# A two-layer graph network on one core: the first layer's table split twice as fast, products from block 12, more early work for GpSimd, the last unit in two

## The chip, the core and the metric

The kernel runs on one core of a Trainium2 chip. A core has five engines that run side by side and meet through semaphores: TensorE (PE; its weight loads are listed as PEld), VectorE (DVE), ScalarE (ACT), GpSimd (POOL) and SyncE (SP, which here only issues transfers). Transfers run on 16 DMA engines. Computing engines read and write the on-chip memory; TensorE's results go to a small memory of accumulators (PSUM).

The metric is the device time of one execution in microseconds (us); lower is better. The profile is one execution on the chip, recorded instruction by instruction.

## What is computed

The input is a graph of 6,250 nodes with 128 features each and 200,000 edges, sorted by destination. Two layers follow each other; each begins with a layer norm and a relu and adds its result to `x`:

```python
h = jnp.maximum(_layernorm(x), 0.0)
# layer 0: attention over the edges
z = h @ W                                   # 128 features in 8 heads of 16
e = leaky_relu(el[src] + er[dst])           # el, er: one number per node and head
a = exp(e - segment_max(e, dst)[dst])
x = x + segment_sum(z[src] * a, dst) / segment_sum(a, dst) + bias
h = jnp.maximum(_layernorm(x), 0.0)
# layer 1: messages weighted by a small network on the edge features
s, v = h[:, :32] @ W_up_s, h[:, 32:] with W_up_v
w0..w3 = split(silu(silu(edge_feats @ A1 + b1) @ A2 + b2) @ A3)
m = concat(s[src]*y_s*w0, (v[src].y_v)/R3*w3, s[src]*y_v*w1, v[src]*y_s*w2)
x = x + (segment_sum(m, dst) / 10) @ W_out
```

The part that matters for the change is `z[src]` in layer 0 and `s[src]`, `v[src]` in layer 1: for each of the 200,000 edges a row of a table is fetched, by an index that only the data tell.

## The kernel before

**Tiles and blocks.** Nodes lie in `NX` = 50 tiles of 128. Edges lie in `TU` = 1563 tiles of 128, sixteen tiles to a block (`KB` = 16), so there are `NB` = 98 blocks; the last has 11 tiles. Since the edges are sorted, the destinations of a block fall into a window of 128 nodes; the sum over edges is a product with a one-hot matrix of the destinations.

**Three ways to fetch rows.** The table of layer 0 is `t0` (136 numbers a row), that of layer 1 is `t1` (128 numbers), both in the chip's main memory.
- Most edge tiles are fetched with an indirect transfer that GpSimd issues (`gather`, line 839): one instruction for 128 rows. Those of a block go into one of five buffers (`buffer()`), which are used in turn; a gather into a buffer has to wait until the block that was there has been read.
- In every third block, tile 15 is fetched row by row by SyncE (`rows_by_row`, line 1154): 128 small copies, whose number per step is paced by `rows_until`.
- In "dense" blocks (`dense` in layer 0, every fourth block, `dense1`, in layer 1) tile 14 (`KD`) is not fetched but computed: a one-hot matrix of the sources (`ends_to`, line 1300) times the whole table (`rows_of` of layer 0, line 1313). For that the table lies on chip, each number split into three bf16 parts (`t0s`). Three tiles of the table at a time (`TS` = 3) are loaded by SyncE (`asked(k)`, line 1275) into one of two buffers `zr` and split by VectorE (`split(k)`, lines 1228 to 1231), k from 0 to 16. The product takes 17 one-hot matrices by 3 parts, 51 matmuls; `taken` (lines 1319 and 1321) picks the result. Its tiles are taken in `order`.

**Prologue.** Line numbers 880 to 1005. GpSimd first gathers rows of the input `x` itself for the first edge tiles (`gather_x`, line 905): `KX` = 25 tiles. Meanwhile the other engines norm the 50 node tiles in ten groups and write `t0` (`rows_of` of the prologue). There the groups' normalising step (line 960) runs on VectorE and ScalarE, except that in two of the groups five tiles are normed by GpSimd (`late`). VectorE then computes whether the edges are evenly spread (`fok`, line 936); every engine reads that number and branches. After the branch `rows_of` runs a second time, over the 25 gathered x tiles, and computes their table rows directly, so these 25 edge tiles need no gather from `t0`.

**Layer 0.** One step `g` a block, in an order written out by hand for TensorE, VectorE, ScalarE and SyncE (`manual_schedule`): gathers of block g+3 are issued, the logits of block g computed, one-hots of blocks g+1 and g+2 prepared, the sums of block g-1 taken, finished node tiles normed and multiplied for layer 1 and written to `t1`. A copy `t1z` of `t1` is written too, with zeros for the last `NL` = 3 node tiles. In step g stand `asked(g - 2)` near the begin and `split(g - 3)` at the end.

**The seam.** Layer 1's gathers need all of `t1`, whose last tiles come at the very end of layer 0. So the first `NE` = 24 edge tiles of layer 1 are gathered early from `t1z`, and the rows of the last three node tiles are added afterwards by a product with a one-hot (`late_ends`, lines 1868 and 1872; `late_rows`, lines 1883 and 1886), four edge tiles at a time.

**Layer 1.** Units of up to four edge tiles (`us`). For each: the small network on TensorE and ScalarE, the messages on VectorE (`messages`, lines 1807 to 1816), the sums on TensorE (line 1824). The last block's 11 tiles make units of 4, 4 and 3. After the last unit come the last two node tiles' products and the write to `out`.

The lines that name the changed numbers:

```python
NL, NE = 3, 24
TS = 3
dense = set(range(-(-NX // TS) + 4, NB - 4))     # 21 .. 93
us = [{"b": b, "k0": k0, "m": min(4, KT[b] - k0)}
      for b in range(NB) for k0 in range(0, KT[b], 4)]
```

Of the kernel before, what the change touches and what calls it, by code (L numbers as in the profile page):

```python
# [13 lines left out]
OP = mybir.AluOpType  # L14
# [15 lines left out]
KB = 16  # L30
# [711 lines left out]
def tile_even_edges(  # L742
# [28 lines left out]
    nc = tc.nc  # L771
    NX = xp.shape[0] // P
    TU = n_tiles
    TG = -(-TU // P)
    NB = -(-TU // KB)
# [27 lines left out]
    src_col = keep.tile([P, TU], I32, name="fsrc")  # L803
    z_first = keep.tile([P, KB, ZW], F32, name="fz_first")
    ok_i = keep.tile([1, 1], I32, name="fok")
    KX = KB + 9
    z_second = keep.tile([P, KB, ZW], F32, name="fz_second")
    other = keep.tile([P, KB, ZW], F32, name="fz_other")
    flat = other.rearrange("p k f -> p (k f)")
# [46 lines left out]
    with tc.manual_schedule(engines={mybir.EngineType.PE, mybir.EngineType.DVE,  # L856
# [11 lines left out]
        xs = [fx.tile([P, n, P], F32, name=f"fxs{i}") for i, n in gx]  # L868
# [69 lines left out]
        def rows_of(gx, xs, fp, fp_ps, raw=None):  # L938

            mark = "e" if raw else ""  # L940
            NC = len(gx)
            mvs, rss, mrs, hs = {}, {}, {}, {}
            todo, done, outs, ers = [], [], [], []
            for k in range(NC + 3):
                if 0 <= k - 1 < NC:
                    rss[k - 1] = deviation(fp, mvs[k - 1], gx[k - 1][1], f"x{mark}{gx[k - 1][0]}")
                c = k - 2
                if 0 <= c < NC:
                    i, n = gx[c]
                    rs, mr = rss[c], mrs[c] = normal(fp, mvs[c], rss[c], n, f"x{mark}{i}")  # L950
                    h = hs[c] = fp.tile([P, 6, P], F32, name="fh")
                    for j in range(n):
                        by = (i + j) % 7
                        if by in ((2, 6) if c < NC - 2 else (2,)):
                            nc.scalar.activation(h[:, j, :], xs[c][:, j, :], AF.Identity,
                                                 bias=mr[:, j, :], scale=rs[:, j, :])
                        else:
                            late = by in (0, 3, 5) and NC - 4 <= c < NC - 2 and not raw
                            eng = nc.gpsimd if late else nc.vector
                            eng.tensor_scalar(h[:, j, :], xs[c][:, j, :], mvs[c][:, j, 0:1],  # L960
                                              rs[:, j, :], op0=OP.subtract, op1=OP.mult)
                if k == NC + 1 and not raw:
                    uneven_edges()
                for i, n, zt in ers:
                    nc.vector.tensor_copy(er_all[:, i : i + n, :], zt[:, :n, ZW:])
                ers = []
                if k >= 3:
                    i, n = gx[k - 3]
                    zt = raw[k - 3] if raw else fp.tile([P, 6, CW], F32, name="zt", bufs=4)
                    todo += [(k - 3, zt, j0, min(3, n - j0)) for j0 in range(0, n, 3)]  # L970
                while todo:
                    c, zt, j0, m = todo.pop(0)
                    p_t = fp_ps.tile([P, 4, P], F32, name="p_t")
                    for j in range(m):
                        nc.tensor.transpose(p_t[:, j, :], hs[c][:, j0 + j, :], ident)
                    h_t = fp.tile([P, 3, P], F32, name="h_t")
                    nc.scalar.activation(h_t[:, :m], p_t[:, :m], AF.Relu)
                    done.append((c, zt, j0, m, h_t))
                    while len(done) > (1 if k < NC + 2 or todo else 0):
                        c, zt, j0, m, h_t = done.pop(0)  # L980
                        p_z = fp_ps.tile([P, 3, CW], F32, name="p_z")
                        for j in range(m):
                            nc.tensor.matmul(p_z[:, j, :], h_t[:, j, :], w_ext, start=True, stop=True)
                        outs.append((c, zt, j0, m, p_z))
                        while len(outs) > (1 if k < NC + 2 or todo or done else 0):
                            c, zt, j0, m, p_z = outs.pop(0)
                            copy = nc.scalar.copy if c < NC - 2 else nc.vector.tensor_copy
                            w = ZW if raw else CW
                            copy(zt[:, j0 : j0 + m, :w], p_z[:, :m, :w])
                            i, n = gx[c]  # L990
                            if j0 + m == n and not raw:
                                to_table(t0, zt[:, :, :ZW], i, n, nc.sync)
                                ers.append((i, n, zt))
                                load(c)
                if k < NC:
                    i, n = gx[k]
                    mvs[k] = moments(fp, xs[k], n, f"x{mark}{i}")
            for i, n, zt in ers:
                nc.vector.tensor_copy(er_all[:, i : i + n, :], zt[:, :n, ZW:])
# [11 lines left out]
def even_edges(tc, v):  # L1011
    nc = tc.nc
    NX, TU, TG, NB, KT, MC = (v[k] for k in (
        "NX", "TU", "TG", "NB", "KT", "MC"))
# [5 lines left out]
    with ExitStack() as ctx:  # L1020
# [25 lines left out]

        NL, NE = 3, 24
        LATE = NX - NL  # L1050
        sv_of = {}
        iota = const.tile([P, P], F32, name="fiota")
# [9 lines left out]
        with tc.tile_pool(name="fbuild", bufs=1) as build:  # L1062
# [30 lines left out]
            for k, by in enumerate((-H, P - H, H)):  # L1093
# [4 lines left out]
                                    op0=OP.mult, op1=OP.add)  # L1098
# [11 lines left out]
            with tc.tile_pool(name="fat_ps", bufs=1, space=PSUM) as at_ps, \  # L1110
                    tc.tile_pool(name="fat_c", bufs=1) as at_c:
                col = at_c.tile([P, P], F32, name="fcol")
                n = NB - 1
# [83 lines left out]
        order = sorted(range(NR), key=lambda k: (k > 0, 2 * NR + k < NX, k))  # L1197
        half = (NR + 1) // 2
        TS = 3
        dense = set(range(-(-NX // TS) + 4, NB - 4))  # L1200
        dense1 = set(range(10, NB - 4, 4))

        ranges = []
# [34 lines left out]
        with tc.manual_schedule(engines=in_order), \  # L1238
# [23 lines left out]
            def asked(k):  # L1262

                i = TS * k
                if 0 <= i < NX:
                    n = min(TS, NX - i)
                    zr = asked.of[k] = l0d.tile([P, TS, ZW], F32, name="zr", bufs=2)[:, :n]
                    if i == 0:
                        nc.vector.memset(zr[:W0, 0, :], 0.0)
                        nc.sync.dma_start(zr[W0:, 0, :], t0[: P - W0, :])  # L1270
                        of = t0[P - W0 : n * P - W0]
                        nc.sync.dma_start(zr[:, 1:], of.rearrange("(j p) f -> p j f", p=P))
                    else:
                        of = t0[i * P - W0 : (i + n) * P - W0]
                        nc.sync.dma_start(zr, of.rearrange("(j p) f -> p j f", p=P))

            def split(k):
                if k in asked.of:
                    zr = asked.of.pop(k)
                    n = min(TS, NX - TS * k)  # L1280
                    in_three(t0s[:, TS * k : TS * k + n], zr, rest0[:, :n])
# [295 lines left out]
            for g in range(NG - 3):  # L1577
# [4 lines left out]
                    node_out(n)  # L1582
                for n in split_:
                    parts_out(n)
                asked(g - 2)
                if g % 2 == 0 and g // 2 + 2 < NX - 2:
                    node_rows(g // 2 + 2, 1)
                rows_until(rows, g + 1)
                c, b4 = cs[g], (cs[g - 1] if g else None)
# [64 lines left out]
                    sums(b4, 8)  # L1654
                if to:
                    rows_of(n2, 6, half - 6)
                split(g - 3)
                if g == 4:
                    ends_in_ranges(const)
                if g == NG - 4:  # L1660
# [74 lines left out]
        with tc.manual_schedule(engines=in_order), \  # L1735
# [192 lines left out]
            def dense_step(b, q):  # L1928
# [6 lines left out]
                if b in dense1:  # L1935
# [4 lines left out]
            blk = [{} for _ in range(NB)]  # L1940
            us = [{"b": b, "k0": k0, "m": min(4, KT[b] - k0)}
                  for b in range(NB) for k0 in range(0, KT[b], 4)]
            NU = len(us)

            def take_rows(b):
# [219 lines left out]
```

## Time and profile before

| | |
|---|---|
| median of 3 runs | 5950.58 us (5947.39 to 5958.39) |
| the profiled execution | 3749.37 us, of which the span from the first to the last instruction is 3747.6 us |
| mean granted TensorE clock in it | 0.936 of full speed |
| row copies of SyncE (line 1154) | 7808, of 0.5 KB |
| moved by DMA | 262.78 MB, 70 GB/s on average |

The profiled execution and the runs differ by 2201 us; every duration in this document that is read from a view belongs to the profiled execution.

How to read the views. The page gives for each engine its busy time and share of the span. Its second part cuts the span in 40 equal slices: a digit is the busy share in tenths; PEclk is TensorE's granted clock in tenths of full speed. A line of groups reads: source line, engine, operation, output<-input by the program's names, count | busy time, mean ns of one | idle time of the engine just before, and who ended it. A line of the timeline reads: start, duration, engine, line, operation, count, and in brackets the idle time before it and its releaser. "issue" means that nothing in the profile was waited for. An "SPq" entry is a transfer being issued, not its data moving.

### The profile page before, as it was taken

The page shows a single profiled execution, that of the slowest core. Times are in us where ns is not written, and L with a number is a line of the kernel's source. Part 1 is how long each engine was busy: PE and PEld are TensorE (multiplying, and loading weights), DVE is VectorE, ACT ScalarE, POOL GpSimd, SP SyncE. Part 2 cuts the span into 40 slices and gives each one's busy share as a digit, 9 for nine tenths or more (in the row PEclk, how much of TensorE's full clock was granted, in tenths as well). Part 3 has the DMA queues.
Part 4 walks back from the last instruction along what each step waited for, and adds up shares of the span by engine and source line. Part 5 has one row for each costly group of instructions (what it writes and reads, how often), then busy time and mean ns, then how long its engine had stood idle before and what let it go on. Part 6 is the DMA issues. An engine that isn't in the chain of part 4 may idle for free. (4 is left out here: it accounts for less than half of the span.)

```text
span 3747.6 us, 74803 instructions
## 1 busy us (share of the span) xinstructions
PE 3196.4 (85%) x19845; PEld 2474.1 (66%) x19845; DVE 2633.1 (70%) x6272; ACT 1406.0 (38%) x3638; POOL 2817.3 (75%) x2981
## 2 busy tenths in 40 slices
PE   4756788888888888888788899999999999999997
PEld 4655566666666666666666677777677777767775
DVE  7755666666666666666657777777777777777776
ACT  4432333333333333333334444444444444444443
POOL 7777777777777777777777777777777777777776
PEclk7766899999999999999799999999999999999999
DMA  6333332222222222222223222222222222222222
GB/s 167 75 78 79 71 68 67 68 69 68 68 68 68 68 68 67 69 69 67 71 70 95 69 64 64 64 64 64 64 64 64 65 63 64 65 63 64 63 68 52
DMA packets 212534, 262.78 MB, mean 70 GB/s; under 512 B 77425, under 2 KB 163921, under 8 KB 212097
## 3 DMA queue, kind: packets, MB, share of 16 engines
q0 software_dynamic: 95072, 200.78, 22.6%
q1 hardware_dynamic: 116592, 57.03, 5.7%
q8 instruction: 159, 2.61, 0.3%
q14 instruction: 279, 2.28, 0.2%
q10 hardware_dynamic: 432, 0.09, 0.0%
HBM read 236.19 MB, written 21.14 MB: 69 GB/s over the span
## 5 line engine op out<-in xcount | busy, mean ns | idle before, releaser
L839 POOL DMA_INDIRECT fz<-ft,fsrc x1750 | 1654.1, 945 | 539.5 <-issue 327.0
L1824 PE MATMUL p_u<-mj,s 128*128 128x256 f32 x3126 | 764.3, 388 | 87.5 <-DVE mj L1816 86.5
L1313 PE MATMUL p_x<-t0s,fz_first 128*128 128x408 bf16 (+1 forms) x3723 | 730.0, 346 | 0.0
L1824 PEld LDWEIGHTS p_u<-mj,s 128*128 128x128 f32 x3126 | 582.2, 192 | 215.6 <-DVE mj L1816 139.7
L839 POOL DMA_INDIRECT fz_other<-ft,fsrc x589 | 557.2, 946 | 179.6 <-issue 107.6
L839 POOL DMA_INDIRECT fz_second<-ft,fsrc x583 | 554.0, 950 | 178.3 <-issue 107.9
L1313 PEld LDWEIGHTS <-fz_first 128*128 128x128 bf16 x3723 | 361.5, 101 | 231.5 <-issue 17.4
L1791 ACT ACTIVATE p_w<-p_w,yb 128x64 f32<-128x64 f32 x1563 | 451.5, 289 | 117.3 <-PE p_w L1787 73.8
L1787 PE MATMUL p_w<-fa3p,h 128*128 128x256 f32 x1564 | 408.4, 384 | 0.0
L1787 PEld LDWEIGHTS p_w<-fa3p,h 128*128 128x128 f32 x1564 | 286.7, 193 | 114.5 <-issue 48.8
L1772 ACT ACTIVATE h<-p_h,fb 128x512 f32<-128x512 f32 x196 | 134.7, 687 | 585.8 <-PE p_h L1770 575.1
L1337 ACT COPY mk<-p_m 128x384 f32<-128x384 f32 (+1 forms) x99 | 47.4, 479 | 658.5 <-PE p_m L1333 651.6
L1427 PE MATMUL p_u<-fz,s 128*128 128x136 f32 x1846 | 272.9, 308 | 20.1 <-DVE fz L1422 20.1
L1427 PEld LDWEIGHTS p_u<-fz,s 128*128 128x128 f32 x1846 | 258.5, 216 | 23.8 <-DVE fz L1422 22.2
L1173 DVE TENSOR_TENSOR s<-p_i,fdloc 128x512 f32<-128x512 f32 x391 | 268.6, 687 | 3.8 <-ACT p_i L1766 3.8
L1173 DVE TENSOR_TENSOR s<-p_m,fdloc 128x512 f32<-128x512 f32 x391 | 266.2, 682 | 3.0 <-ACT mk L1337 2.7
L1770 PE MATMUL p_h<-ft,fa1p 128*128 128x128 f32 x1568 | 216.1, 282 | 56.5 <-DMA ft<-in_e_f_dram 56.3
L1770 PEld LDWEIGHTS p_h<-ft,fa1p 128*128 128x128 f32 x1568 | 208.7, 197 | 79.8 <-issue 55.7
L1348 ACT CAST d<-p_d 128x512 bf16<-128x512 f32 x391 | 229.3, 586 | 78.0 <-PE p_d L1346 34.2
L1378 DVE TENSOR_TENSOR_SCAN pe<-mk,pe 128x128 f32<-128x128 f32 x98 | 42.0, 428 | 290.8 <-PE pe L1293 271.6
L1777 ACT ACTIVATE h<-p_h,fb 128x512 f32<-128x512 f32 x196 | 134.7, 687 | 260.4 <-PE p_h L1774 260.4
L1811 DVE TENSOR_REDUCE vd<-vy 128x128 f32<-128x384 f32 x391 | 229.6, 587 | 0.0
(285 smaller groups left out, 4880.5 us busy)
## 6 DMA issues: line engine op xcount, KB each, us to landing
r<-ft SPq DMA_DIRECT2D x3968, 0.5 KB
r<-ft SPq DMA_DIRECT2D x3840, 0.5 KB
fz<-ft,fsrc POOLq DMA_INDIRECT x1750
fz_other<-ft,fsrc POOLq DMA_INDIRECT x589
fz_second<-ft,fsrc POOLq DMA_INDIRECT x583
fx<-x SPq DMA_DIRECT2D x47, 160.0 KB
ft<-in_e_f_dram SPq DMA_DIRECT2D x98, 64.0 KB
t1s<-fx SPq DMA_DIRECT2D x7, 576.0 KB
```

The costliest lines, as they stand in the source:

```text
L839: nc.gpsimd.indirect_dma_start(out=to[:, k, :width], out_offset=None, in_=table, in_offset=bass.IndirectOffsetOnAxis(ap=src_col[:, t : t + ...
L1173: nc.vector.tensor_tensor(s[:, :m], iota[:, None, :].to_broadcast([P, m, P]), dloc[:, t : t + m].unsqueeze(2).to_broadcast([P, m, P]), OP. ...
L1313: nc.tensor.matmul(c["p_x"][:, :m, :], c["oh", k // half][:, k % half, :], t0s[:, i::NR, s, :], start=k == 0 and s == 0, stop=k == NR - 1 ...
L1348: nc.scalar.copy(d[:, :m], p_d[:, :m])
L1427: nc.tensor.matmul(c["p_u"][:, :ZW], c["s"][k // 4][:, k % 4, :], c["z"][:, k, :], start=c["o"] + k == 0, stop=c["o"] + k == KT[c["b"]] - 1)
L1770: nc.tensor.matmul(p_h[:, q, :], a1p[:, q0 + q, :], c["ft"], start=True, stop=True)
L1772: nc.scalar.activation(c["h1"], p_h, AF.Silu, bias=b1)
L1777: nc.scalar.activation(h2, p_h, AF.Silu, bias=b2)
L1787: nc.tensor.matmul(w[:, k : k + n].rearrange("p k a u -> p (k a u)"), c["h2"][q // 4][:, q % 4, :], a3p[:, :n].rearrange("p k f -> p (k f) ...
L1791: nc.scalar.activation(w[:, k, ::2, :], w[:, k, ::2, :], AF.Copy, scale=c["yb"][:, k0 + k, 0:1])
L1811: nc.vector.tensor_reduce(vd, vy.rearrange("p t i u -> p t u i"), AX.X, OP.add)
L1824: nc.tensor.matmul(blk[b]["p_u"][:, :MW], u["s"][:, k, :], u["mj"][:, k, :], start=k0 + k == 0, stop=k0 + k == KT[b] - 1)
```

## The change

`KX` goes from 25 to 29 and `NE` from 24 to 28. In the prologue's normalising step the GpSimd branch is gone; VectorE does those five tiles. `dense` begins at block 12 instead of 21. To have the table ready, a step calls `asked` twice and `split` twice, with the same two indices, 2g-4 and 2g-3, so that a piece is loaded at the begin and split at the end of the same step. The last unit of layer 1, of three tiles, is cut into one of two tiles and one of one. Three operations of the gather count change with it: 1422 instead of 1435 gathers from `t0`, 28 instead of 24 from `t1z`, 1483 instead of 1487 from `t1`; and 29 instead of 25 gathers of x.

```diff
-    KX = KB + 9
+    KX = KB + 13
...
                         else:
-                            late = by in (0, 3, 5) and NC - 4 <= c < NC - 2 and not raw
-                            eng = nc.gpsimd if late else nc.vector
-                            eng.tensor_scalar(h[:, j, :], xs[c][:, j, :], mvs[c][:, j, 0:1],
-                                              rs[:, j, :], op0=OP.subtract, op1=OP.mult)
+                            nc.vector.tensor_scalar(h[:, j, :], xs[c][:, j, :], mvs[c][:, j, 0:1],
+                                                    rs[:, j, :], op0=OP.subtract, op1=OP.mult)
...
-        NL, NE = 3, 24
+        NL, NE = 3, 28
...
         TS = 3
-        dense = set(range(-(-NX // TS) + 4, NB - 4))
+        dense = set(range(-(-NX // TS // 2) + 3, NB - 4))
...
-                asked(g - 2)
+                for k in range(2):
+                    asked(2 * g - 4 + k)
...
-                split(g - 3)
+                for k in range(2):
+                    split(2 * g - 4 + k)
...
+            if us[-1]["m"] > 2:
+
+                n = us[-1]["m"] - 2
+                us[-1]["m"] = 2
+                us.append({"b": NB - 1, "k0": us[-1]["k0"] + 2, "m": n})
             NU = len(us)
```

## The prediction

> **What bounds the kernel now.** I read the page first: engine shares, the row of slices, the costliest groups. Then GpSimd's (POOL's) timeline around the prologue and the seam between the layers, the busy time in stretches of the first layer, VectorE's timeline inside one step, and the tail.
>
> From the page (the groups' columns are count | busy, mean ns | idle before, its releaser):
>
> ```profile
> span 3747.6 us, 74803 instructions
> PE 3196.4 (85%) x19845; PEld 2474.1 (66%) x19845; DVE 2633.1 (70%) x6272; ACT 1406.0 (38%) x3638; POOL 2817.3 (75%) x2981
> ...
> POOL 7777777777777777777777777777777777777776
> PEclk7766899999999999999799999999999999999999
> ...
> L839 POOL DMA_INDIRECT fz<-ft,fsrc x1750 | 1654.1, 945 | 539.5 <-issue 327.0
> ```
>
> TensorE's 85% is the larger share, but POOL's row is flat from end to end: the same 7 in every slice, whatever the other engines do. One gather takes 0.945 us and a fixed 0.30 us of issue follows. From 41.17 to 3733 us the gathers start every 1.25 us, and the waits of POOL show one gap over 1 us there, at the seam. There are 1435 gathers from the first table, 24 early ones and 1487 from the second by the program's loops (the page's groups hold 2938 of the 2946; a few records are missing): 2946 x 1.25 = 3682 us, the span but for the prologue (41), the tail (14) and a few long gathers. So in this execution POOL paces everything.
>
> POOL's timeline in the prologue and at the seam (start, duration, instruction, idle before):
>
> ```profile
> 22.70 0.94 POOL L905 DMA_INDIRECT fz_first<-in_e_xp_dram,frow  x1 [0.30 <-issue]
> 24.10 4.21 POOL L960 TENSOR_SCALAR fh<-fxs,mvx,rsx 128x128 f32<-128x128 f32 x5 [0.46 <-PE p_t L975]
> 28.47 1.03 POOL L905 DMA_INDIRECT fz_second<-in_e_xp_dram,frow  x1 [0.16 <-issue]
> ...
> 39.41 0.94 POOL L905 DMA_INDIRECT fz_second<-in_e_xp_dram,frow  x1 [0.30 <-issue]
> 41.17 0.98 POOL L839 DMA_INDIRECT fz_second<-ft,fsrc  x1 [0.82 <-issue]
> ```
>
> ```profile
> 1868.22 1.08 POOL L839 DMA_INDIRECT fz<-ft1z,fsrc  x1 [0.30 <-PE p_n L1481]
> 1869.61 0.94 POOL L839 DMA_INDIRECT fz<-ft1z,fsrc  x1 [0.31 <-issue]
> 1876.60 0.94 POOL L839 DMA_INDIRECT fz<-ft,fsrc  x1 [6.04 <-PE p_h L1868]
> ```
>
> The reader should see 4.21 us of layer norm inside POOL's stream, and 6.04 us in which POOL stands still after the 24th early gather, until the second table is whole.
>
> Busy time in a stretch without products and one with them (us, then busy and count of PE, PEld, DVE, ACT, POOL, then clock):
>
> ```profile
> 180.00:260.00 80.00, 46.03 (x318) 41.37 (x319) 48.90 (x113) 25.24 (x58) 60.47 (x65) 0.67 0.34 77
> 440.00:540.00 100.00, 89.47 (x695) 66.24 (x694) 68.14 (x142) 30.11 (x70) 75.62 (x80) 0.95 0.30 67
> ```
>
> POOL is busy 0.756 of both; TensorE goes from 0.58 to 0.89, its clock from 0.67 to 0.95. Inside a step before block 21, VectorE waits for gathered rows right after the table split:
>
> ```profile
> 363.36 0.58 DVE L1231 TENSOR_TENSOR t0s<-rest,t0s 128x408 bf16<-128x408 f32 x1
> 370.44 0.29 DVE L1369 TENSOR_TENSOR e_s<-fz,p_er 128x128 f32<-128x128 f32 x1 [6.50 <-DMA fz<-ft,fsrc]
> ```
>
> **The median is another matter.** The profiled execution took 3749.37 us (span 3747.6 and 1.8 around it); the median of the runs is 5950.58, 1.587 times as long, and no view says where the other 2201 us lie. I make the sum against 3749.37 and ask afterwards which engine can be the pace at 5950.
>
> **What the Trainium skill says.** "GPSIMD Engine Reference", section 4, names gathers with data-dependent indices as work for GpSimd alone, whose cores write the descriptors in software. The trace agrees: each gather holds POOL for 0.945 us. "SBUF — State Buffer", "Who interferes with whom", says that a VectorE tensor_scalar can enter a mode in which it locks GpSimd out of a shared port for the whole instruction. The moved layer norm is of that kind, but the gathers between 12.67 and 20.19 us, beside VectorE's own L960, take 0.94 to 0.98, so I charge nothing. "TensorE: Matmul & The Clock Gate", Part 1, says that TensorE's clock is half unless sustained activity releases it; the two stretches above, 0.67 and 0.95, agree.
>
> **The change part by part.**
>
> Products from block 12. The set of dense blocks goes from 21..93 to 12..93: nine blocks more take tile 14 from products with the split table instead of a gather. POOL loses 9 x 1.25 = 11.2 us. TensorE gains in each 51 matmuls of L1313 (730.0 us / 73 blocks = 10.0 us) and a spread; VectorE gains the one-hots L1300 (1.36 + 1.22) and the taking (3 x 0.36), 3.7 us. A dense block's POOL period is 14.67 gathers x 1.25 = 18.3 us; TensorE needs 0.895 of that, 16.4 us at clock 0.95, and in blocks 21 to 93 POOL never waits beside that same load. Hidden, if the clock is granted. Without that cover, at 0.67, it is 23.3 us a block: rival A.
>
> Split at double rate. Nothing is added in all: the same 17 pieces, of 4 x 0.58 us on VectorE, in steps 2 to 10 instead of 3 to 19. Per step 2.4 us come on top and fall into the 4 to 6.5 us wait shown above. A piece is now loaded and split in the same step. SyncE issues the load once the last step's splits are done (the issues at 117.0, 134.0, 154.3 show it), about 17 us before the split at the step's end, so it is there in time. On SyncE's queue the second load takes 0.41 us; behind it stand the row copies, 44 in 17.6 us, and between them the queue has free 2 to 3 us in every three steps. Hidden.
>
> Prologue. Five operations leave POOL: 24.10 to 28.47 becomes free, and four more x gathers (4 x 1.25 = 5.0) fill it. These end at 23.9 + 13 x 1.25 = 40.2 instead of 40.35, and four table gathers fewer follow: 5.0 us gained. VectorE takes the five at 0.34, pipelined 0.27: 1.4 us, so its verdict on the edges (ends at 37.25) comes at 38.6 and its last table copy as much later. The first table gather waits for both; at 41.17 there is room for the first, for the second perhaps not: I take 0 and keep 1 us. VectorE, ScalarE and TensorE norm four more x tiles and one more group, about 4 us, so block 0 starts 5 us later. What is late next is buffer reuse: block 6 overwrites block 1's buffer, free at 119.9, wanted at 133.1. After it: free at 125, wanted at 128. Three us are left; block 7 has 147 against 142 once the doubled splits are counted.
>
> Seam. Four more gathers need only the zero-padded table: 5.0 of the 5.7 us of extra wait are filled. The cost: one more round of late ends and rows, 16 matmuls of 0.275 (4.4 us) and VectorE's 3 x 0.74 + 0.69 = 2.9 us. Block 2's buffer was last read at 1967.4 and wanted again at 1984; the margin of 16 shrinks to about 5. Hidden.
>
> Last unit in two. The unit of three tiles takes VectorE 2.3 us after the last gather lands; in two it costs about 0.6 us more in instructions and leaves two matmuls instead of six behind. I take 0 (-0.5 to +0.5).
>
> Sum: 11.2 + 5.0 + 5.0 = 21.2 us off 3749.4, 3728.2 (-0.57%), with 16 to 22 as bounds.
>
> **Carried to the median.** If POOL is stretched to the longer run, a gather takes (5950 - 55)/2946 = 2.0 us; 13 gathers fewer are 26 us, and the seam has no wait left to fill, since 24 x 2.0 exceeds the 36 us from the last first-layer gather (1840) to the second table. If the excess is a constant, 21 us. By ratio, 34. I take 26: 5925 us; this case's own range is 5912 to 5936.
>
> **Rivals.**
>
> A, slower: TensorE is the pace. For it: busy 3196.4 at mean clock 0.936 is 2992 us at full clock, and twice that, at half clock, is 5984, within 1% of the median. Against it: the profile's clock. The place is blocks 12 to 20, and it decides once a dense block's 15.6 us (at full clock) exceed 18.3, at a clock under 0.85. If only those blocks stay at 0.67, each takes 23.3 instead of 19.6 us: 9 x 3.7 = 33, less the 10 of prologue and seam, +23 us, 5975. At half clock throughout, 9 x 10.0 x 0.95 x 2 = +171 at most; less what waits hide, about +150: 6100.
>
> B, no change: the row copies on SyncE are the pace of the longer run. There are 7808 of them, 0.40 us each here; at 0.76 they alone would fill 5950. The change removes none. For it: SyncE has little slack here. Against it: nothing shows it stretched. Time 5950, to 5945.
>
> C, given back: the buffer of block 1 isn't free (if block 0 starts 9 rather than 5 us late, POOL stands 1 to 5 us), the first table gather comes 1 us later, and the tail costs 0.5. Gain 15 in this execution's time, 5936.
>
> That the change doesn't do what it says: the table's last piece (tiles 48, 49) is split in step 10, and block 12's products with it come in step 11; I see no way for that.
>
> **How the numbers follow.** Forecast 0.58, C 0.06, B 0.11, A 0.25 (of it 0.09 near 5975, 0.16 higher). About 0.2% (12 us) is what a measurement of this kernel tells from no change: the forecast and C count as faster, 0.64, B as same with a little of A, 0.12, the rest slower, 0.24. The range reaches from the ratio's end, with a margin, over B and A's lower end: 5905 to 5995; A's upper end is left out.
>
> **What would show it.** Right: 1422 gathers from the first table, still one every 1.25 us, the first near 41, none standing over 1 us at the seam, the clock near 0.95 from about 220 us instead of 420, and the last gather 21 us earlier. Wrong: a gap on POOL at blocks 6 to 8; idle on POOL behind L1313 or L1427 in blocks 12 to 20; VectorE waiting on L1228 for a load; a profiled gain near 21 with a longer median, which would make A or B the pace of the timed runs.

## The result, and the profile after

The changed kernel takes 5976.21 us (median of 8 runs, 5956.22 to 5984.85); the kernel before took 5948.81 us (8 runs, the three from ahead of the prediction among them). The ratio is 1.0042, with a 95% interval of 1.0024 to 1.0060: slower by about 25 us, where 5925 us and a gain were forecast.

The profiled execution of before that the prediction rests on (3749 us) was not a luckier run of the same thing: this kernel takes about 3746 us on some chips and 5890 to 5960 us on others, and in each later comparison the kernel before keeps to one of the two paces. (Each chip was seen in one comparison only; on which chips the first profile and the first runs were made is not on record.) I call them the short and the long pace. The result above was measured at the long pace, the profile that I argued from at the short one.

From the page of the changed kernel (5984.85 us; groups: count | busy, mean ns | idle before, releaser):

```profile
span 5983.1 us, 75909 instructions
PE 3890.7 (65%) x20366; PEld 2776.4 (46%) x20366; DVE 2667.2 (45%) x6346; ACT 1393.8 (23%) x3643; POOL 2807.6 (47%) x2967
...
POOL 6344444444444444444444455555545555545552
PEclk7667777777777777777766888888888888888889
...
L839 POOL DMA_INDIRECT fz<-ft,fsrc x1740 | 1648.1, 947 | 1828.4 <-PE p_u L1425 654.5
```

A gather still takes 0.947 us. But GpSimd's row has fallen from 7 to 4, and the gathers of this group wait 1828 us instead of 540. The largest part with a name, 654 us, is for the first layer's sums (L1425) to give a buffer back. The gathers are not stretched; GpSimd stands still. So the two pages can't be set side by side, and the kernel before has to be profiled at the long pace first.

### The profile page after: what moved, and what is told of

It reads as the page before. It is cut to its first block, busy times and chain, and to the rows that moved or that the text cites. A ratio compares the mean times of both kernels' runs of the same rounds, so it can differ in the third digit from the quotient of the medians.

```text
span 5983.1 us, 75909 instructions
## 1 busy us (share of the span) xinstructions
PE 3890.7 (65%) x20366; PEld 2776.4 (46%) x20366; DVE 2667.2 (45%) x6346; ACT 1393.8 (23%) x3643; POOL 2807.6 (47%) x2967
## 3 DMA queue, kind: packets, MB, share of 16 engines
q8 instruction: 163, 2.67, 0.2%
## 5 line engine op out<-in xcount | busy, mean ns | idle before, releaser
L1311 PE MATMUL p_x<-t0s,fz_first 128*128 128x408 bf16 (+1 forms) x4182 | 1087.7, 398 | 495.5 <-issue 494.8
L1824 PE MATMUL p_u<-mj,s 128*128 128x256 f32 x3126 | 881.1, 430 | 334.7 <-DVE mj L1816 239.1
L1824 PEld LDWEIGHTS p_u<-mj,s 128*128 128x128 f32 x3126 | 651.9, 216 | 507.4 <-DVE mj L1816 285.4
L1311 PEld LDWEIGHTS <-fz_first 128*128 128x128 bf16 x4182 | 441.5, 110 | 945.8 <-issue 807.1
L1787 PE MATMUL p_w<-fa3p,h 128*128 128x256 f32 x1564 | 446.2, 412 | 0.6 <-issue 0.6
L1774 PE MATMUL p_h<-h,fa2p 128*128 128x512 f32 x392 | 247.2, 718 | 220.1 <-ACT h L1772 217.0
L1787 PEld LDWEIGHTS p_w<-fa3p,h 128*128 128x128 f32 x1564 | 315.4, 212 | 146.2 <-issue 106.9
L1770 PE MATMUL p_h<-ft,fa1p 128*128 128x128 f32 x1568 | 237.0, 300 | 119.5 <-DMA ft<-in_e_f_dram 104.1
L1770 PEld LDWEIGHTS p_h<-ft,fa1p 128*128 128x128 f32 x1568 | 233.7, 216 | 144.6 <-issue 122.7
L1425 PE MATMUL p_u<-fz,s 128*128 128x136 f32 x1846 | 258.8, 298 | 19.4 <-DVE fz L1420 19.4
L1917 PE MATMUL p_x<-t1s,ohs 128*128 128x384 bf16 x1071 | 208.5, 343 | 73.4 <-DVE ohs L1907 58.1
```

The lines of the kernel that those rows point to most:

```text
L1311: nc.tensor.matmul(c["p_x"][:, :m, :], c["oh", k // half][:, k % half, :], t0s[:, i::NR, s, :], start=k == 0 and s == 0, stop=k == NR - 1 ...
L1425: nc.tensor.matmul(c["p_u"][:, :ZW], c["s"][k // 4][:, k % 4, :], c["z"][:, k, :], start=c["o"] + k == 0, stop=c["o"] + k == KT[c["b"]] - 1)
L1770: nc.tensor.matmul(p_h[:, q, :], a1p[:, q0 + q, :], c["ft"], start=True, stop=True)
L1774: nc.tensor.matmul(p_h.rearrange("p q e -> p (q e)"), a2p, c["h1"].rearrange("p q e -> p (q e)"), start=True, stop=True)
L1787: nc.tensor.matmul(w[:, k : k + n].rearrange("p k a u -> p (k a u)"), c["h2"][q // 4][:, q % 4, :], a3p[:, :n].rearrange("p k f -> p (k f) ...
L1824: nc.tensor.matmul(blk[b]["p_u"][:, :MW], u["s"][:, k, :], u["mj"][:, k, :], start=k0 + k == 0, stop=k0 + k == KT[b] - 1)
```

## The experiments

Lines of code are those of each kernel; the changed kernel's L1311 and L1425 are L1313 and L1427 before. The chips differed from group to group, so each ratio is taken against the kernel before on the same chip.

### Each part alone, and the products taken away (short pace)

e0 is the kernel before, unchanged. e1 is before with the first part alone:

```diff
-        dense = set(range(-(-NX // TS) + 4, NB - 4))
+        dense = set(range(-(-NX // TS // 2) + 3, NB - 4))
...
-                asked(g - 2)
+                for k in range(2):
+                    asked(2 * g - 4 + k)
...
-                split(g - 3)
+                for k in range(2):
+                    split(2 * g - 4 + k)
```

e2 is the changed kernel with these lines turned back. e3 is before with `dense = set()`. The expectations set the prediction's theory against a new one: in the trace of the changed kernel, TensorE's instructions often start one by one, 0.70 us apart, ahead of a fetch of instructions.

> The kernel before, unchanged, for a profile of an execution as long as the timed runs (about 5950 us; the profile of before that the prediction was made from took 3749). Supply theory (the trace of the changed kernel shows stretches in which TensorE's instructions start one by one every 0.70 us, about 16 of them before each fetch of 256 instructions): the same stretches here, about one in 256 TensorE instructions, absent in the 3749 us profile; blocks with products start about every 31.5 us, blocks without them about every 29. GpSimd theory (the prediction's): the gather itself or its issue is longer than 1.25 us here. Clock theory (rival A): no such stretches, matmuls back to back at a lower clock.

> Before plus the first part alone: products from block 12, table split at double rate (932 TensorE instructions more, 9 gathers fewer). Supply theory: 932/256 = 3.6 more stalls of 11.3 us, partly hidden, so about +25 us (+10 to +45), which is all of the change's loss. GpSimd theory: -11 to -18 us. Clock theory: +25 us or more, as 9 blocks at half clock.

> The changed kernel with products from block 21 and the split at single rate again, so prologue, seam and last unit only. Supply theory: GpSimd stands idle half of the time in the long runs, so what is taken from it is worth nothing: 0 us (-8 to +6). GpSimd theory: -10 us or more. Clock theory: 0.

> Before without any products in the first layer: tile 14 is gathered in all 98 blocks (73 gathers more, 7555 TensorE instructions fewer by the program's listing); the split table is still made. Output unchanged. Supply theory: 73 blocks go from 31.5 to about 29 us, -180 us, up to 7555/256 x 11.3 = -330 if TensorE is the pace in the others too. GpSimd theory: +91 us (73 x 1.25) to +146 (73 x 2.0). Clock theory: products hold TensorE for 1088/4182 = 0.26 us each at the end of the long profile's busy count, so -970 us or more from 3723 of them.

Before took 3746.05 us here (22 runs): the short pace. e0, profiled, took 3752.91.

```
e1  products and split alone      3731.06 us   ratio 0.9963 (0.9950 to 0.9977)   -15.0 us
e2  prologue, seam, last unit     3738.48 us   ratio 0.9979 (0.9970 to 0.9987)    -7.6 us
e3  none in the first layer       3832.68 us   ratio 1.0232 (1.0217 to 1.0248)   +86.6 us
```

e1 lies where the GpSimd theory put it (-11 to -18). e2 and e3 stay a little short of it (-10 or more, +91 or more), and e2 lies in the supply theory's range too (-8 to +6), but e1 and e3 don't: 86.6 us for 73 gathers is 1.19 us a gather. At the short pace GpSimd sets the time. The supply and clock theories were made for the long pace, which this comparison did not meet. e0 showed none of the 0.70 us stretches, and nothing of the long pace.

### The same kernel and three cuts (long pace)

e4 is the changed kernel itself. e5 has `dense = set()` and `dense1 = set()`. e6 leaves out the row copies:

```diff
-            by_row = [list(range(6 - 3 * i, NB - 2, 3)) for i in range(2)]
+            by_row = [[], []]
```

e7 takes the products with the table's first bf16 part alone, so that the other two parts are left out:

```diff
-                    for s in range(3):
+                    for s in range(1):
...
-                                         stop=k == NR - 1 and s == 2)
+                                         stop=k == NR - 1 and s == 0)
```

> The changed kernel, unchanged. If the kernel before takes about 3746 us here, as in the four runs before this: -15 (products alone) and -7.6 (all but products) add up to -22.6 us, ratio 0.994, GpSimd's flat 1.25 us per gather to the end. If the kernel before takes about 5950: +25 us again, ratio 1.004. A third theory, that the changed kernel brings the long executions on by itself: about 5976 beside a before of 3746.

> The changed kernel without products in either layer (82 and 21 blocks; 10650 TensorE instructions fewer by the listing, 103 gathers more); tables still split, output unchanged. Where before takes 3746: GpSimd theory +103 x 1.25 = +129 on the changed kernel, +106 against before. Where before takes 5950: supply theory 82 x 2.5 = -205 in the first layer (31.5 to 29 us a block) and something in the second, -200 to -470 against before; GpSimd theory +150 to +200.

> The changed kernel with no rows copied one by one on SyncE: tile 15 is gathered in all blocks (61 gathers more, 7808 copies and as many moves fewer on SyncE); output unchanged. Where before takes 3746: +61 x 1.25 = +76 on the changed kernel, +54 against before. Where before takes 5950: rival B (SyncE's copies pace the long executions, its instructions too start one by one there) -100 us or more; supply theory with TensorE as the one that lags -20 to +10; GpSimd theory +90.

> The changed kernel with the first layer's products from the table's first bf16 part alone (17 pairs of weight load and matmul a block in place of 51, 5576 instructions fewer; the two remainders of the table are left out of the products). Gathers unchanged. Where before takes 3746: hidden anyway, 0 (-4 to +4) on the changed kernel; if TensorE's time were paid there, -20 or more. Where before takes 5950: supply theory 5576/256 x 11.3 us = -246 us at most, -100 to -246 on the changed kernel.

Before took 5957.84 us here (27 runs).

```
e4  the changed kernel            5976.01 us   ratio 1.0037 (1.0022 to 1.0052)
e5  no products at all            5910.24 us   ratio 0.9931 (0.9907 to 0.9956)   -66 us on e4
e6  no row copies                 5865.60 us   ratio 0.9850 (0.9827 to 0.9874)  -110 us on e4
e7  one of three parts            5924.19 us   ratio 0.9942 (0.9926 to 0.9958)   -52 us on e4
```

This fells three theories at once, all of them about the long pace. GpSimd as the pace wanted e5 150 to 200 us slower; it is faster, with 103 gathers more. TensorE's clock or its array as the pace (rival A) wanted many hundred off e5; it got 48 off before, with TensorE busy 49% of the span. And the supply theory wanted 200 to 470 off e5 and 100 to 246 off e7, which gave 48 and 52. "Runtime: NRT & Kernel Launch", "Instruction fetch mechanics", in the Trainium skill says that instructions are streamed in blocks of 256 and that the fetch is mostly hidden; the block size agrees with the trace of the changed kernel (163 packets of 2.67 MB together, about 16,384 bytes each, on queue q8, for 20366 matmuls and as many weight loads: 250 to a packet). In e5 TensorE's one-by-one starts in the first layer's blocks are gone while its time hardly fell, so they were a sign and not what the kernel waited for. Whether something of the kind holds other engines stays open: SyncE's row copies are still slow there beside gathers (12 in 9.24 us, 0.77 each).

e6 gave on e4 what its expectation asked of rival B, 100 us or more. But the copies can't be what sets the pace: with none left, the time is still 5866 us.

VectorE's timeline in e5, where no product stands in the way, shows what is left (start, duration, instruction, idle before and its releaser):

```profile
1518.58 0.68 DVE L1171 TENSOR_TENSOR s<-p_m,fdloc 128x512 f32<-128x512 f32 x1
1537.19 0.43 DVE L1376 TENSOR_TENSOR_SCAN pe<-mk,pe 128x128 f32<-128x128 f32 x1 [17.93 <-remote]
```

VectorE waits 17.9 us, for a release that the trace can't name. The gathers of that run go from 1515.74 to 1536.70: it ends when they end.

### Before at the long pace: what happens while gathers run

> The kernel before, unchanged, for a profile where it takes about 5900 to 5960 us. Supply theory: TensorE's one-by-one stretches before each fetch, one in 256 instructions. Theory of the gathers (other engines crawl from 3 us after a run of gathers begins to its end): 20 us runs of gathers with 9 to 11 us pauses; first block's sums start near 194 us (204 in the changed kernel); blocks 12 to 20 take about 30 us each against the changed kernel's 31.5, the seam and the second layer alike. If before takes 3746: as in the first profile.

The kernel before, profiled at 5886.61 us on a third chip. First its page, then GpSimd's timeline with the gathers between left out, and SyncE's:

```profile
span 5884.6 us, 74803 instructions
PE 3729.2 (63%) x19845; PEld 2715.7 (46%) x19845; DVE 2630.0 (45%) x6272; ACT 1393.0 (24%) x3638; POOL 2823.6 (48%) x2981
...
L839 POOL DMA_INDIRECT fz<-ft,fsrc x1750 | 1657.2, 947 | 1762.2 <-PE p_u L1427 683.6
```

```profile
1499.00 0.94 POOL L839 DMA_INDIRECT fz<-ft,fsrc  x1 [12.68 <-PE p_u L1427]
...
1515.25 0.95 POOL L839 DMA_INDIRECT fz<-ft,fsrc  x1 [0.30 <-issue]
1529.88 0.95 POOL L839 DMA_INDIRECT fz<-ft,fsrc  x1 [13.68 <-PE p_u L1427]
```

```profile
1491.52 8.11 SPq L1154 DMA_DIRECT2D r<-ft  x24
...
1500.26 24.72 SPq L1154 DMA_DIRECT2D r<-ft  x40
```

Busy time in three stretches of it: the end of a pause, the gathers from 4 us after their start to 3 us after their end, and the pause that follows (us, then busy and count of PE, PEld, DVE, ACT, POOL, then clock, DMA share, GB/s):

```profile
1489.00:1503.00 14.00, 12.15 (x88) 8.55 (x89) 11.36 (x23) 4.49 (x11) 3.08 (x4) 0.83 0.09 24
1503.00:1519.00 16.00, 7.19 (x39) 3.80 (x37) 0.00 (x0) 0.00 (x0) 10.15 (x11) 0.75 0.25 54
1519.00:1530.00 11.00, 9.02 (x63) 6.20 (x64) 8.68 (x20) 5.39 (x12) 0.12 (x1) 0.75 0.01 1
```

And TensorE and VectorE inside the middle stretch, each from its own timeline:

```profile
1505.15 0.27 PE L1372 MATMUL pe<-fident,e_s 128*128 128x128 f32 x1
...
1507.58 0.33 PE L1313 MATMUL p_x<-t0s,fz_first 128*128 128x408 bf16 x1 [0.68 <-issue]
1508.28 0.33 PE L1313 MATMUL p_x<-t0s,fz_first 128*128 128x408 bf16 x1 [0.38 <-issue]
1509.70 0.33 PE L1313 MATMUL p_x<-t0s,fz_first 128*128 128x408 bf16 x1 [1.08 <-issue]
```

```profile
1501.31 0.68 DVE L1173 TENSOR_TENSOR s<-p_m,fdloc 128x512 f32<-128x512 f32 x1
1519.06 0.43 DVE L1378 TENSOR_TENSOR_SCAN pe<-mk,pe 128x128 f32<-128x128 f32 x1 [17.06 <-remote]
```

For comparison, 40 us of e0, the same kernel at the short pace, in which the gathers start every 1.25 us without a pause:

```profile
1000.00:1040.00 40.00, 35.66 (x273) 25.87 (x272) 27.84 (x57) 11.71 (x28) 30.24 (x33) 0.93 0.26 67
```

The reader should see one thing from five sides. For 16 us VectorE and ScalarE start nothing. TensorE's transpose L1372, for which the scan L1378 waits, runs at 1505.15, and the scan starts at 1519.06. TensorE itself steps by 0.7 us and multiples of it. A row copy on SyncE takes 0.34 us in the pause (8.11/24) and 0.62 on average over the stretch that has the gathers in it (24.72/40). Within 3 us of the last gather's end (1516.20) all go on together, and GpSimd waits 13.7 us for their buffers. So a block is its gathers and then the work of the others, hardly overlapped, where at the short pace the two run side by side (VectorE is busy 27.8 of the 40 us in e0). It isn't bandwidth: 54 GB/s here, 67 there.

This block is not an exception. Counted over e12's first layer from 250 us on (90 runs of gathers), VectorE starts 0.13 instructions a us from 4 us after a run's begin to its end, and 1.5 in the pauses. The second layer is different: 1.1 against 1.5, as in this stretch, where VectorE works on beside nine gathers:

```profile
4020.00:4031.00 11.00, 7.02 (x34) 5.37 (x32) 4.18 (x11) 1.84 (x5) 8.52 (x9) 0.95 0.22 56
```

Of the 2134 us by which e12's span exceeds e0's, about 1277 pass before the sums of the first layer's last block and 857 after. How the second layer loses its part was not followed.

The Trainium skill, "SBUF — State Buffer", "Who interferes with whom", has a port that VectorE and GpSimd share and that one of them can lock, and says that a DMA never contends with a compute engine. A lock of that kind can't be all of it: ScalarE, TensorE and SyncE are held too. Whether, against that sentence, the gathers' DMAs hold them, no run shows. What is held, an instruction's start or the news that its input is ready, the trace can't settle: it has 22,393 records of DMAs raising semaphores here and 70,302 in e0 for the same program, and the release is put down as "remote". Whether the recording itself, which loses so much at the long pace, has a part in the hold-up was not tested either.

### Gathers spaced out (long pace)

If the gathers hold the others up, spacing them should help, though it only adds work to GpSimd. e10 puts three memsets of its destination ahead of each gather, e14 one:

```diff
             k = first + t - tiles[0]
+            for _ in range(3):
+                nc.gpsimd.memset(to[:, k, :width], 0.0)
             nc.gpsimd.indirect_dma_start(
```

e11 is the changed kernel without products and without row copies, e15 that with one memset a gather.

> The changed kernel with three memsets of each gather's destination on GpSimd ahead of the gather (8800 memsets more; output unchanged). At an estimated 0.2 to 0.4 us each they stretch a gather's period from 1.25 to 1.9 to 2.4 us. Where before takes 3746: GpSimd is the pace, +1800 to +3400 us. Where before takes about 5955: if gathers hold the other engines up (this theory), those get on during the memsets, and the time rises by far less than the memsets' sum, +0 to +1000; if it is only that buffers come late and the two alternate whatever GpSimd does, +1800 to +3400 there too.

> The changed kernel without any products and without row copies (164 gathers more than the changed kernel). Where before takes 3746: +164 x 1.25 = +205 on the changed kernel, +182 against before. Where before takes about 5955: the sum of the two runs there, -48 and -92 against before plus the changed kernel's +18: about -158, 5800.

> The changed kernel with one memset of each gather's destination ahead of the gather, a period of about 1.25 + 0.25 = 1.5 us. Where before takes about 5950: if what frees the other engines grows with the spacing, between the changed kernel (+20) and three memsets (-369): about -150; if any break in the run is enough, GpSimd is the pace at 1.5 us, 2937 x 1.5 + 200 = 4600, -1300. Where before takes 3746: 2937 x 0.25 = +730 us.

> No products, no row copies and one memset ahead of each gather (3100 gathers). Where before takes about 5950: lower than 5446 (the same without memsets) if spacing helps whatever the others have to do, about 5100; GpSimd's floor is 3100 x 1.5 + 200 = 4850. If it is slower than 5446, the spacing only pays where the row copies and products are. Where before takes 3746: 3100 x 1.5 + 60 = 4710, +960.

```
                                               before there    ratio
e10  three memsets a gather      5537.91 us     5906.58   0.9378 (0.9354 to 0.9402)
e11  no products, no rows        5446.32 us     5906.58   0.9212 (0.9184 to 0.9240)
e14  one memset a gather         5702.25 us     5913.47   0.9643 (0.9613 to 0.9672)
e15  e11 with one memset         5169.31 us     5913.47   0.8737 (0.8709 to 0.8765)
```

8800 needless instructions on GpSimd make the changed kernel 6% faster than the kernel before. My own theory had allowed 0 to +1000 us for e10 and forecast no gain. GpSimd's timeline in e10, and VectorE's beside it:

```profile
1511.49 0.38 POOL L840 MEMSET fz<- 128x136 f32 x2
1512.03 0.95 POOL L841 DMA_INDIRECT fz<-ft,fsrc  x1 [0.16 <-POOL fz L840]
1512.98 0.68 POOL L840 MEMSET fz<- 128x136 f32 x4
1514.14 0.95 POOL L841 DMA_INDIRECT fz<-ft,fsrc  x1 [0.48 <-POOL fz L840]
```

```profile
1512.60 0.43 DVE L1378 TENSOR_TENSOR_SCAN pe<-mk,pe 128x128 f32<-128x128 f32 x1 [0.39 <-PE pe L1293]
```

The gathers start every 1.8 us on average, and they no longer come in runs with pauses. The scan that had waited 17 us starts while a gather is still on GpSimd, 0.9 us after its transpose (L1372 at 1511.66), where that took 13.9 us in e12. VectorE now waits for gathered rows instead, 2042 us in all (L1369 and L1809), and the last gather starts 13 us before the end of the span, 86 in e12. So with three memsets GpSimd sets the pace again, and still more of them should cost time. The theory that the buffers alone make GpSimd and the others alternate wanted 1800 us more. One memset, a period of 1.37 us within a run, gives -211 (-150 was forecast), so from none to three the gain grows with the spacing. What the runs don't part is the spacing from the memset itself.

e11 was forecast at 5800 as the sum of e5 and e6, and took 5446. With only one of the two cut, the first layer's blocks from block 12 on take 30.3 us (e5) or 32.0 (e6); with both, 27.5. Why the two together free so much more was not settled.

### The parts at the long pace

e8 is the changed kernel, e9 has e1's code and e13 e2's.

> The changed kernel, unchanged, once more. Where before takes about 3746 us: -22.6 us (the sum of the two parts measured there), ratio 0.994. Where before takes about 5955: +22 us again, ratio 1.004.

> Before plus products from block 12 and the split at double rate. Where before takes 3746: -15 us again. Where before takes about 5955, the theory now is that there the other engines nearly stand still while GpSimd's gathers run (from 3 us after the first gather of a block to the last one, SyncE falls from 4.7 to 1.4 instructions a us, VectorE and ScalarE to almost none), so that a block takes its gathers and then the rest of the work after one another; 9 blocks then save 1.25 us of gathers and pay for 51 weight loads and matmuls: 31.4 - 28.9 = 2.5 us more each, +22 us, all of the change's loss. Rival (the loss comes from prologue or seam, where GpSimd stood still for 61 us at block 6): 0 or less.

> The changed kernel with products from block 21 and the split at single rate. Where before takes about 5950: +10 us, because the first block starts 10 us later (204 against 194) and nothing makes it up, with +5 to +28 as bounds (28 is what 44 less 16 leaves). Rival: 0, since the parts differ by noise. Where before takes 3746: -7.6 us again.

```
                                  before there    ratio
e8   the changed kernel            5906.58   1.0081 (1.0055 to 1.0106)
e9   products and split alone      5906.58   1.0027 (1.0013 to 1.0042)   +16 us
e13  prologue, seam, last unit     5913.47   1.0016 (1.0002 to 1.0031)    +9 us
```

The sum, +25, is what the first comparison found. But the two parts were measured on two chips, the second is barely clear of nothing (+1 to +18), and the whole varies in size, though not in sign at this pace (e4 +18, e8 +44; +22 to +25 was forecast): on e9's own chip, e8 leaves 28 us for what e9 doesn't contain. Where the loss arises, by the times at which a block's first sums start in the traces (us from the span's start):

```
                        block 0   block 12   block 21   end
before (e12)              195       530        802      5885
all but products (e13)    202       538        811      5894
products alone (e9)       194       543        831      5959
changed kernel (e8)       204       547        830      5928
changed (first profile)   204       548        834      5983
changed (e4)              203       553        837      5985
```

Block 0 starts 7 to 9 us later wherever the prologue is changed (e13 too, e9 not). GpSimd's timeline shows where: in e12 its own normalising (L960) breaks its row of x gathers, and the first gather from the table comes at 55 us; in the changed kernel the x gathers run on to 39 us without a break, and the table is ready later:

```profile
22.77 0.95 POOL L905 DMA_INDIRECT fz_first<-in_e_xp_dram,frow  x1 [0.30 <-issue]
34.15 4.21 POOL L960 TENSOR_SCALAR fh<-fxs,mvx,rsx 128x128 f32<-128x128 f32 x5 [10.43 <-PE p_t L975]
...
55.38 2.35 POOL L839 DMA_INDIRECT fz_second<-ft,fsrc  x1 [4.97 <-DVE frest L1068]
```

```profile
69.08 1.61 POOL L839 DMA_INDIRECT fz_second<-ft,fsrc  x1 [29.16 <-DMA ft<-zt]
```

It is 68 to 70 us in all four profiles with the changed prologue (the first of the changed kernel, e4, e8, e13) and 55 in the two without (e9, e12). That fits gathers that hold the others up, since the break is gone, but no run puts the break alone back.

The steps with the doubled split (up to block 12) take 344 to 350 us instead of 335 or 336, and blocks 12 to 20 with products take 282 to 288 instead of 272 or 274. No run parts the split from the products. Between two profiles the ends differ by more than the change does, so the last column proves little; the first three agree in all six. Busy time in blocks 12 to 20 of e12, then of the first profile of the changed kernel:

```profile
530.00:802.00 272.00, 129.85 (x865) 100.90 (x865) 109.89 (x239) 55.21 (x124) 129.52 (x136) 0.67 0.20 46
```

```profile
548.00:834.00 286.00, 194.07 (x1164) 126.42 (x1165) 115.71 (x241) 53.24 (x121) 124.88 (x132) 0.77 0.17 40
```

GpSimd is busy 4.6 us less there (132 instructions instead of 136: the other gathers saved are issued outside the stretch) and TensorE 64 us more, at a clock that rose from 0.67 to 0.77. Gathers were saved; the stretch got 14 us longer.

### The changed kernel at the short pace, and the best version there

e17 is e15 with two memsets.

> The changed kernel, unchanged. Where before takes about 3746: -22.6 us, ratio 0.994. Where before takes about 5900 to 5960: +25 us (products +16, prologue +9), ratio 1.004.

> No products, no row copies and two memsets ahead of each gather. Where before takes about 5900: the period goes from 1.37 to about 1.6 us, GpSimd's floor to 3100 x 1.6 + 200 = 5160; others get on a little better: 5100 to 5250, so no clear gain on 5169. If the others were still the ones waited for at one memset, below 5100. Where before takes 3746: 3100 x 1.6 + 60 = 5020.

This comparison fell on a chip with the short pace: before 3745.55 us (23 runs). The changed kernel took 3735.53 us (20 runs, 3726.61 to 3753.62), ratio 0.9969 (0.9958 to 0.9981), -10 us: a gain, half of the forecast 21. e17 took 5240.85, ratio 1.398 (5020 was forecast): there GpSimd is the pace, without a gap over 3.1 us in its waits, and a version made for the long pace loses 40%. e15 beats the kernel before by 13% where that takes 5913; at the short pace e1's products alone do as well as the whole change (0.9963 and 0.9969). No version here is best at both.

From the page of e16, then GpSimd's timeline at the end of its prologue and at the seam:

```profile
span 3733.6 us, 75909 instructions
...
POOL 7777777777777777777677777777777777777776
PEclk7679999999999999999799999999999999999999
```

```profile
42.70 0.94 POOL L839 DMA_INDIRECT fz_second<-ft,fsrc  x1 [2.06 <-DMA ft<-zt]
```

```profile
1825.27 0.94 POOL L839 DMA_INDIRECT fz_first<-ft1z,fsrc  x1 [3.30 <-DMA ft1z<-sv]
...
1865.62 0.95 POOL L839 DMA_INDIRECT fz<-ft,fsrc  x1 [5.67 <-PE p_h L1868]
```

## Why the prediction was wrong

**What bounds the kernel.** Right at the short pace (e3: 1.19 us a gather), wrong at the long one, where GpSimd is busy 48% (e12).

**The sum of 21.2 us.** For the execution that it was made against it had the right sign, and twice the size: -10 us (-15.7 to -7.1). The products, put at -11.2, gave -15.0 alone (e1), and prologue and seam, put at -10, gave -7.6 (e2). Together they gave less than their sum. In e16's profile the term that was mis-sized is the seam: four more early tiles were to fill 5.0 of the 5.7 us of extra wait, and 5.67 us of idle stand there still, with 3.30 more ahead of the first early gather, whose zero-padded table isn't whole yet (0.30 of each is the usual issue time). In e1 and in e2 the gathers from the second table follow the early ones after 0.30 us. So each part alone already removed the seam's wait, the sum counts it twice, and with both GpSimd comes to the seam too early for the others: its last gather from the first table starts at 1821 us, against 1827 in e1, 1835 in e2 and 1841 in e0. The first table gather came 1.5 us later than in the first profile of before (42.70 against 41.17), where I took nothing and allowed for one. As forecast, the gathers run on past blocks 6 to 8 without a gap. The clock is granted earlier, though later than forecast: it is 0.97 from 260 us on, where 220 was named, against 0.93 from 420 us on in the first profile of before. The last gather starts 20 us earlier than in e0 (3715.95 against 3735.95); the tail behind it grew from 15.1 to 17.7 us, where the last unit was put at nothing.

**The step that failed** is "Carried to the median": "If POOL is stretched to the longer run, a gather takes (5950 - 55)/2946 = 2.0 us; 13 gathers fewer are 26 us". No gather is stretched: it takes 947 ns at 5885 us and 945 at 3748. The excess is time in which GpSimd waits for the others (1762 us ahead of one group of gathers in e12, 540 in the first profile), and in the first layer the others had all but stood still while it gathered. There a gather saved isn't 2.0 us won, nor does a constant excess, the other reading in that paragraph, leave the 21 us: 103 gathers more in place of the products made the kernel faster (e5). And what is called hidden isn't hidden. Products and doubled split cost 16 us (e9), and prologue, seam and last unit cost 9 (e13): the first gather from the table, whose delay was taken as 0 and allowed 1 us, comes 13 to 15 us later. I divided a time that no view showed among the gathers, because they were the pace of another, shorter execution.

**Rival A** gave 5975 us, and 5976.21 came. Its sign and a part of its place were right, its mechanism was not, so the number is luck. It asked for TensorE as the pace in blocks 12 to 20, with the clock left at 0.67, 3.7 us more in each; they cost 1.2 to 1.9, at a higher clock than before (0.77), and without any product the kernel gained 1% instead of the many that the pace would have to give (e5). The rest of the loss lies in the prologue and the doubled split, where A counted a gain of 10 us. **Rival B** named SyncE's copies: leaving them out is worth 110 us (e6), but they aren't the pace either. **Rival C**, the gain partly given back, is what happened at the short pace, though mostly at the seam and not at block 1's buffer.

The chance of 0.24 for slower was too low for what the profile could support. 3749 against 5950 was in plain sight, and a profile of one doesn't speak for the other.

## What to carry to other kernels

Before a profile is used, set its time beside the runs: if they differ by a third, nothing in it tells which engine paces the runs, and a profile at their pace comes first. An engine that "works beside" another in one profile may be held up by it on the next chip; a long row of gathers on GpSimd is worth testing with a small filler between them, which costs one line and showed here that the others got on when the gathers were spaced. Work counted as hidden is hidden only at the pace at which it was seen so.

## What the runs showed that I had not expected

The kernel before takes 3746 us on two chips and 5907 to 5958 on three others, with equal busy times on GpSimd (2822 and 2824 us in e0 and e12), VectorE (2633 and 2630) and ScalarE (1406 and 1393). On these three engines the difference is waiting alone (TensorE is busy 3729 us against 3196, at a lower clock), and in the first layer it lies where gathers follow one another at 1.25 us. At the long pace, three memsets of 0.22 us ahead of each gather made the changed kernel 369 us quicker than before's 5907, and one memset, without products and row copies, 744 quicker than 5913. What makes the two paces, which resource the gathers take from the others, and what lengthens the second layer stay open.
